# Half-width products: two PSUM sums in one bank, the second value mix in the freed one, and a new order of work

## The chip, the cores and the metric

One core of one Trainium2 chip. The metric is the device time of one execution in microseconds; lower is better. Three runs of the kernel before give a median of 2415.76 us (2412.73 to 2417.64).

## The reference

128 graphs ("batches") of 128 nodes with 512 features pass through two layers. Each ends in a residual and a layer norm without parameters (eps 1e-5).

```python
# layer 0: multi-head attention, 8 heads of 64, masked by the adjacency
q = inputs @ Wq + bq;  k = inputs @ Wk + bk;  v = inputs @ Wv + bv
logits = einsum('bqhd,bkhd->bhqk', q, k) / sqrt(64)
attn = softmax(where(adj > 0, logits, -1e9))
x = layernorm(x + relu(einsum('bhqk,bkhd->bqhd', attn, v) @ Wo + bo))
# layer 1: graph attention with one edge score per pair of nodes
Wh = x @ W;  e = leaky_relu((Wh @ a1)[:, :, None] + (Wh @ a2)[:, None, :], 0.2)
attention = softmax(where(adj == 0, -1e9, e), axis=2)
x = layernorm(x + elu(attention @ Wh))
```

Everything is float32. The value returned is x after layer 1, shape 128 x 128 x 512.

## The kernel before

**Tiling.** Batches are worked on in 64 pairs. The five big products are those with Wq and Wk (together "qk"), Wv ("v"), Wo ("o") and W ("w"). Each is done for a pair at once as a 2 x 2 block product with seven instead of eight block multiplications: the seven products of a family are numbered j = 0 to 6 in `PRODUCTS`, and each adds into one of three PSUM sums, A (j = 0, 2), B (j = 1, 3, 5) and C (j = 4, 6). This text writes A0 and A1, B5, B6 and B3, C4 and C7 for them, after the sum and the left block. Left blocks 4 to 7 are sums made by `left_sums` on POOL (`x_sums`, `o_sums`, `z_sums`; tiles sx, so, sz).

Between the products of one sum an engine reads it: after A0 comes `p1` (tile e1a or e1b), after A1 `c11`; after B5 `p6` (u2), after B6 `p7` (u3), after B3 `c21`; after C4 `c22`, after C7 `c12`. The next product into that sum waits for its reader. In v and w the readers of A are on ScalarE, all others of the half-width families on VectorE. The qk sums are 512 columns wide and fill a PSUM bank of 128 x 512 float32. The sums of v, o and w are 256 columns wide.

**PSUM.** Eight banks. The pool `ps_att` holds the logits of two batches, two banks each (tile s). The pool `ps_acc` has the tags accA, accB and accC, one bank each, which all four families use in turn; a half-width sum has a bank to itself and leaves half of it empty. The pool `ps` has one bank, for both value mixes of a pair (`mix_values`, tile po) and both node mixes (`mix_nodes`, tile pz), one after the other.

**The attention path of a batch**: logits (TensorE), `mask_logits` and `max_logits` (VectorE), `exp_logits` and `norm_logits` (ScalarE, eight instructions each), `weights_t` (VectorE transposes blocks of 32 into tile prb), `weights_out` and `weights_in` (to DRAM, tile prd, and back transposed, tile prT), `mix_values` (TensorE), `mix_values_out` (ScalarE, tile oT). The graph path: `edge_term` and `edge_blocks` (VectorE), `edge_row` (a DMA spreads a row over all partitions, tile ejr), `edge_sums` (ScalarE), `edge_leaky`, `edge_mask`, `edge_max` (VectorE), `edge_exp` (ScalarE), `edges_t` with its way through DRAM (atb, atd, attT), `mix_nodes`, then the w product, `elu_exp`, `elu_low`, `elu_max`, residual, norm, `store`.

**The order of the work** is written out: every step has a due time in `PLAN`, a pair adds `PERIOD`, `ENDS` adds a shift for the first three and the last four pairs, and all steps are issued in the order of the sums. Each engine runs its instructions in that order and waits where data or a buffer is not ready. `GOING` adds matmuls on the identity near the end, whose result nobody reads (`keep_going_late`).

```python
shift = ENDS.get(p if p < n_pair // 2 else p - n_pair, {}).get(key, 0.0)
events.append((p * PERIOD + PLAN[key] + shift, len(events), fn, args))
```

**The start.** Pair 0 uses plain products for qk (`qk_plain`). `weight_sums` makes the four summed weight blocks of each family (wqk and wv on VectorE, wo and w on POOL). `fold_a` multiplies W with a, so that the edge scores come straight from x; it loads each half of a as a_bc (256 KB, spread over the partitions) on POOL's queue when its turn comes, and `fold_t` and `fold_out` spread the result over the partitions.

**The end.** The last pair does o and w with plain products (`plain_product`), reloads the weight rows which the sums have overwritten (rows_o, rows_w), and transposes its softmax weights on TensorE (ppT, pat).

`BUFS` is the number of buffers of each SBUF tag.

Of the kernel before, what the change touches and what calls it, by code (L numbers as in the profile page):

```python
# [8 lines left out]
F32 = mybir.dt.float32  # L9
# [8 lines left out]
PERIOD = 78.768558  # L18
PLAN = dict(
    load_adj=-214.2762, load_blocks=-156.4567, sums_qk=-119.9046, x_transpose0=-118.9579, sums_v=-112.8775,  # L20
    x_transpose1=-64.055, sums_fold1=-60.5833, sums_fold_t1=-41.0724, sums_fold0=-37.6761, sums_fold_out1=-36.5398,
    qk0=-36.0224, x_sums=-35.8404, qk1=-32.9779, qk_p1=-31.7105, fill_logits0=-31.5232, sums_fold_t0=-29.2377,
    qk4=-28.6459, qk_p6=-28.5331, qk_p1q=-27.7049, qk2=-26.3155, qk_c11=-24.8916, qk3=-22.6254, v0=-21.402,
    qk_p7=-19.9439, qk_c22=-19.9339, qk5=-14.7467, qk6=-13.4439, qk_c21=-7.8856, qk_c12=-7.8498, v_p1=-4.7268,
    v1=-4.5449, fill_logits1=-1.8505, mask=-1.2435, v_p6=-0.2943, logits=0.0, sums_fold_out0=0.6684,
    mask_logits0=1.9952, max_logits0=3.7429, v3=4.4065, v_p7=4.433, v2=7.4467, v_c11=9.2069, v4=9.2085,
    mask_logits1=10.0374, load_x1=10.3213, v5=13.2871, v_c22=14.6665, exp_logits0=14.7511, v_c21=15.0921,
    v6=17.2266, v_c12=17.5754, max_logits1=22.1216, sums_o=22.3895, sum_logits0=24.0633, norm_logits0=27.409,
    exp_logits1=33.3029, weights_t0=43.7048, sum_logits1=43.7767, norm_logits1=52.0118, weights_out0=53.6197,
    weights_t1=55.6065, weights_out1=68.011, weights_in0=70.4393, weights_in1=74.301, mix_values0=75.8522,  # L30
    mix_values_out0=80.7212, mix_values1=81.4334, mix_values_out1=85.4398, load_x0=87.1711, sums_w=90.2554,
    o_sums=101.6394, o0=106.2181, o_p1=113.6365, o1=113.6652, o4=115.875, o_p6=116.2192, o_p1l=117.1503,
    o3=117.1603, o_p7=117.3205, o2=117.7709, o_c11=118.2449, o_c22=118.2872, o5=120.8539, o6=121.6955,
    o_c21=121.8792, residual01=122.7569, o_c12=122.7614, stats01=122.8191, mean01=123.8502, residual00=127.7304,
    rstd01=128.2803, shift01=128.7729, stats00=130.3078, norm01=131.2371, mean00=131.4538, rstd00=133.9815,
    edge_term01=134.3884, shift00=135.5918, edge_term11=137.3863, norm00=140.4496, edge_term10=144.2793,
    edge_blocks=146.1519, fill_edges=152.9599, edge_row=155.4786, edge_term00=159.9559, edge_sums=163.3873,
    edge_leaky=169.0665, edge_mask=174.9959, edge_max=179.2956, edge_exp=184.846, edges_t=185.9311,
    edges_t_out=188.282, edges_t_in=189.7663, mix_nodes1=211.95, mix_nodes_out1=218.2462, mix_nodes0=220.5122,
    mix_nodes_out0=222.7905, z_sums=231.0565, w0=248.2279, edge_norm=250.3865, w_p1=253.8429, w1=254.0225,  # L40
    w2=254.7456, w_p6=256.7486, w3=258.7144, w_c11=259.1252, w4=262.9461, w_p7=264.5461, w5=268.1992,
    w_c22=268.2862, w6=268.4953, w_c21=269.0061, w_c12=270.9016, elu_exp1=288.3615, elu_exp0=298.9658,
    elu_low1=307.1177, elu_max1=314.1197, elu_low0=326.1878, elu_max0=338.6625, residual10=340.2052,
    stats10=349.6362, mean10=349.9591, residual11=350.8328, rstd10=358.934, stats11=386.2458, mean11=395.8811,
    shift10=413.3316, rstd11=414.603, shift11=416.7025, finish0=436.5642, finish1=440.8676, store0=451.5942,
    store1=492.1186, tail_exp=492.2186, tail_max=492.3186, tail_sum=492.4186, tail_norm=492.5186)

ENDS = {
    0: dict(
        qk_p1=-693.3008, qk_p1q=-562.1962, qk_p6=-558.7086, qk0=-497.8592, x_transpose1=-494.0942,  # L50
        x_transpose0=-448.1221, fill_logits0=-367.3107, load_x1=-359.65, qk1=-335.4701, qk2=-331.5901,
        load_adj=-316.9328, load_blocks=-299.7933, qk_c11=-289.6601, tail_max=-280.732, mask=-257.6647, qk3=-220.34,
        fill_logits1=-212.9934, qk_c21=-211.3615, fill_edges=-182.6923, qk_c12=-180.0174, x_sums=-178.1562,
        logits=-170.7364, qk_c22=-165.6554, load_x0=-157.2757, qk5=-129.4956, exp_logits0=-115.2104,
        weights_out0=-114.1682, max_logits0=-113.2581, mask_logits1=-111.564, mask_logits0=-111.5243, v4=-108.9856,
        weights_t0=-107.8966, weights_in0=-106.3568, v1=-104.9602, v3=-103.5122, v_p6=-102.5092,
        sum_logits0=-99.1902, v_p1=-98.6495, v2=-98.1896, v_c22=-97.279, v_p7=-96.9685, v6=-95.93,
        max_logits1=-92.4852, v_c11=-92.0931, norm_logits0=-91.8454, v5=-91.0373, weights_t1=-89.8414, v0=-89.7163,
        norm_logits1=-87.923, sum_logits1=-87.4384, v_c12=-84.3643, exp_logits1=-84.0508, v_c21=-82.1213,
        weights_in1=-81.3671, weights_out1=-75.5973, mix_values0=-73.0572, o_sums=-72.5018,  # L60
        mix_values_out0=-71.3249, stats11=-70.0451, mix_values_out1=-68.3664, o0=-68.2642, mix_values1=-65.5116,
        o_p1l=-63.5095, o1=-61.1023, o_p1=-60.89, qk_p7=-54.0233, mean11=-52.6597, o2=-52.1908, o_p6=-51.8324,
        o3=-51.3338, o5=-49.9351, o_p7=-47.5345, o_c11=-46.8, o_c22=-46.5822, o6=-46.5728, residual11=-45.7167,
        o4=-45.2658, o_c21=-41.1905, store1=-37.7402, residual01=-37.493, elu_low0=-36.3281, residual00=-34.7161,
        stats01=-31.1527, stats00=-30.3568, o_c12=-30.2986, elu_low1=-29.8226, elu_exp0=-28.3417,
        edge_term10=-25.0922, norm00=-23.3134, mean00=-22.364, elu_exp1=-20.4366, elu_max1=-19.6739,
        shift00=-19.0277, rstd00=-18.0188, edge_max=-12.5663, edge_mask=-9.2627, edge_norm=-8.9206, mean01=-8.3685,
        w4=-8.2022, shift01=-8.0908, rstd01=-7.6618, mix_nodes1=-7.0678, edges_t=-6.1798, edge_exp=-5.696,
        edge_term00=-5.0867, edges_t_out=-4.9358, edge_leaky=-4.1925, mix_nodes0=-3.6711, mix_nodes_out1=-3.3264,
        w_c22=-2.764, w5=-2.6295, w6=-2.2085, w_p1=-1.9921, w_c21=-1.864, mix_nodes_out0=-1.4624, w_c12=-0.5349,  # L70
        w_p7=-0.4357, w1=-0.3674, edge_sums=-0.3649, finish1=-0.2784, edge_row=0.4769, w_p6=1.2165,
        edge_blocks=1.691, w_c11=1.7828, w3=2.1516, w0=2.4355, w2=2.5822, elu_max0=4.042, rstd11=4.5885,
        edge_term11=7.4074, norm01=8.5979, shift10=10.18, residual10=10.2246, edge_term01=10.4225, z_sums=13.5305,
        qk4=14.4327, edges_t_in=14.663, shift11=23.8601, stats10=33.5595, finish0=35.2453, store0=36.1082,
        rstd10=37.0667, mean10=39.7004, tail_exp=66.8184, tail_norm=66.9674, tail_sum=88.0048, qk6=88.4639),
    1: dict(
        tail_norm=-490.1808, tail_max=-153.045, load_x1=-116.7791, qk_p1q=-113.1873, qk0=-111.5532, qk_p1=-110.0434,
        qk4=-107.6095, qk2=-106.2391, qk3=-105.0977, x_sums=-102.7439, qk1=-102.1183, fill_logits0=-100.8075,
        qk_p6=-100.3165, qk_c11=-99.2056, qk_p7=-95.9145, v0=-95.2879, x_transpose1=-94.0568, v_p1=-93.2182,
        fill_logits1=-91.2167, qk5=-91.0325, qk_c22=-87.7854, qk_c21=-86.0555, mask=-83.9068, qk6=-74.9886,  # L80
        qk_c12=-72.8526, v1=-72.8444, max_logits1=-71.4972, v_p6=-70.6212, v4=-66.8154, v2=-66.3646,
        logits=-65.0664, mask_logits0=-65.0249, mask_logits1=-64.5572, v3=-63.432, exp_logits1=-63.0166,
        max_logits0=-62.096, v_c22=-61.3606, v_c11=-59.6449, v5=-58.7736, v_p7=-55.6045, elu_max0=-48.704,
        v6=-46.8286, v_c21=-46.2548, sum_logits0=-46.1168, residual10=-45.9116, elu_low0=-45.8965,
        exp_logits0=-45.0705, norm_logits0=-44.0432, v_c12=-37.6454, weights_in0=-36.7489, edge_norm=-35.6444,
# [150 lines left out]
BUFS = dict(  # L236
    xb=2, adj=5, xT=3, sx=1, pr=2, qT=2, kT=2, t=2, scr=1, cw=6, e1a256=1, mask=2, u2256=1, u3256=1, cv=2, x=3,
    prb=1, e1a512=1, e1b512=1, u2512=1, u3512=1, prT=2, oT=2, so=1, e1b256=1, co=6, at=1, ejr=1, e=1, atb=1, attT=1,
    zT=2, sz=1)


@with_exitstack
# [841 lines left out]
```

## Time and profile before

| | us |
|---|---|
| median of 3 runs | 2415.76 |
| the profiled execution | 2416.63 |
| its span, first to last instruction | 2414.8 |
| TensorE busy in the span | 2379.1 |
| VectorE / ScalarE / POOL busy | 1859.3 / 1557.8 / 1414.3 |
| granted TensorE clock, mean | 0.998 |

The span lies inside the execution's own time, 1.8 us below it. Busy times of one engine do not overlap with themselves, so span minus busy is what the engine stood idle. A group of matmuls overlaps its successor by its drain: the time it costs is from its start to the next start. One half product is four matmul records (two blocks, each in two passes), a qk product sixteen.

### The profile page before, as it was taken

To read this page: it belongs to the slowest core of one execution; us is meant where nothing else is said; L and a number is where in the kernel's file an instruction comes from. 1 tells how busy PE (TensorE), PEld (TensorE's weight loads), DVE (VectorE), ACT (ScalarE), POOL (GpSimd) and SP (SyncE) were. 2 spreads that over 40 slices of the span, in tenths; PEclk is the share of its full clock that TensorE was granted. 3 is DMA by queue.
4 is the path that set the end of the run, shared out by engine and by line. 5 is a ranking of instruction groups with operands and counts; after the bars stand their busy time and mean duration, and the time that the engine had idled before them with its cause. 6 is when DMAs were issued, how large, how long until landed. Compare 5 with 4: busy or idle time off the path is not lost.

```text
span 2414.8 us, 51884 instructions
## 1 busy us (share of the span) xinstructions
PE 2379.1 (99%) x17768; PEld 2147.7 (89%) x17768; DVE 1859.3 (77%) x3883; ACT 1557.8 (65%) x5512; POOL 1414.3 (59%) x1990
## 2 busy tenths in 40 slices
PE   8999999999999999999999999999999999999997
PEld 7889989989899899899899898998998998998885
DVE  5777777877877877777777778778778777777776
ACT  4656766766766666666667667666666666676664
POOL 3446665655556565665656555565566656555557
PEclk9999999999999999999999999999999999999999
DMA  8435445344344444454443443444444544534333
GB/s 194 114 67 130 112 105 131 101 118 123 104 123 116 112 123 115 101 134 109 108 132 101 117 123 103 123 117 112 123 115 101 134 110 108 134 98 116 109 85 81
DMA packets 341382, 276.59 MB, mean 115 GB/s; under 512 B 126400, under 2 KB 288960, under 8 KB 341120
## 3 DMA queue, kind: packets, MB, share of 16 engines
q1 hardware_dynamic: 339568, 271.17, 43.7%
q8 instruction: 142, 2.33, 0.4%
q10 hardware_dynamic: 1216, 1.31, 0.3%
q0 software_dynamic: 336, 0.79, 0.2%
q14 instruction: 120, 0.98, 0.1%
HBM read 156.90 MB, written 107.87 MB: 110 GB/s over the span
## 4 chain that ended last, share of the span: by engine, by line
PE 92%; DMA 3%; DVE 2%; ACT 2%; SPq 1%; issue 0%; POOL 0%; POOLq 0%; ACTq 0%; DVEq 0%
PE pBqk L486 14%; PE pCqk L486 9%; PE pAqk L486 9%; PE pBv L475 7%; PE pBo L475 7%; PE pBw L475 7%; PE po L804 5%; PE s L731 5%; PE pAo L475 4%; PE pz L914 4%; PE pCw L475 4%; PE pCo L475 4%; PE pAv L475 4%; PE pCv L475 4%; PE pAw L475 4%; DMA ejr<-ej 1%
## 5 line engine op out<-in xcount | busy, mean ns | idle before, releaser
L754 ACT ACTIVATE pr<-pr,nmax 128x128 f32<-128x128 f32 x1024 | 395.3, 390 | 4.0 <-DVE nmax L748 4.0
L763 ACT ACTIVATE pr<-pr,tot 128x128 f32<-128x128 f32 x1024 | 314.5, 411 | 49.8 <-DVE tot L758 49.6
L813 ACT ACTIVATE oT<-po,bv 128x128 f32<-128x128 f32 x512 | 145.0, 364 | 286.0 <-PE po L804 286.0
L956 POOL TENSOR_TENSOR cw<-cw,co 128x512 f32<-128x512 f32 x126 | 159.5, 1285 | 227.1 <-DVE cw L950 227.1
L513 POOL TENSOR_SCALAR rstd<-mv 128x1 f32<-128x1 f32 x255 | 97.6, 383 | 270.4 <-DVE mv L508 261.1
L945 POOL TENSOR_SCALAR t<-t 128x512 f32<-128x512 f32 x126 | 246.9, 1960 | 13.2 <-ACT t L941 13.1
L486 PE MATMUL pBqk<-sx,wqk 128*128 128x128 f32 x2016 | 245.6, 275 | 0.5 <-DVE tot L758 0.5
L486 PE MATMUL pCqk<-sx,wqk 128*128 128x128 f32 x2016 | 246.0, 275 | 0.0
L486 PE MATMUL pAqk<-xT,wqk 128*128 128x128 f32 x2016 | 245.5, 275 | 0.0
L486 PEld LDWEIGHTS pBqk<-sx,wqk 128*128 128x128 f32 x2016 | 239.8, 192 | 3.8 <-issue 0.6
L486 PEld LDWEIGHTS pAqk<-xT,wqk 128*128 128x128 f32 x2016 | 236.3, 192 | 7.0
L486 PEld LDWEIGHTS pCqk<-sx,wqk 128*128 128x128 f32 x2016 | 235.9, 192 | 0.2
L739 POOL MEMSET pr<- 128x1024 f32 x128 | 121.8, 953 | 134.4 <-DVE prb L773 129.8
L743 DVE COPY_PREDICATED pr<-mask,s 128x1024 f32<-128x1024 int32 x128 | 171.0, 1337 | 33.7 <-PE s L731 32.5
L835 DVE SCALAR_TENSOR_TENSOR scr<-co,wa_bc 128x512 f32<-128x512 f32 x256 | 186.3, 728 | 11.3 <-ACT co L523 5.7
L754 ACT ACTIVATION_READ_ACCUMULATOR pr<-pr,nmax 128x1 f32 x1024 | 193.8, 189 | 0.0
L773 DVE STREAM_TRANSPOSE prb<-pr 128x1024 f32<-128x1024 f32 x126 | 156.1, 1239 | 20.2 <-ACT pr L763 19.8
L514 POOL TENSOR_TENSOR rstd<-rstd,half 128x1 f32<-128x1 f32 x255 | 144.7, 567 | 21.2
L748 DVE TENSOR_REDUCE nmax<-pr 128x8 f32<-128x1024 f32 x128 | 155.3, 1213 | 0.2
L804 PE MATMUL po<-prT,cv 128*64 128x128 f32 x2048 | 140.2, 279 | 2.8 <-DMA prT<-prd 2.8
L919 ACT COPY zT<-pz 128x512 f32<-128x512 f32 x128 | 75.9, 593 | 100.8 <-PE pz L914 100.8
L475 PE MATMUL pBv<-wv,sx 128*128 128x256 f32 x512 | 138.0, 392 | 2.4 <-DVE u2v L679 1.3
(198 smaller groups left out, 5982.6 us busy)
## 6 DMA issues: line engine op xcount, KB each, us to landing
prd<-prb SPq DMA_DIRECT2D x126, 512.0 KB, 2.9
prT<-prd SPq DMA_DIRECT2D x504, 128.0 KB, 3.6
x<-in_x_dram SPq DMA_DIRECT2D x128, 256.0 KB, 4.2
out_dram<-cw SPq DMA_DIRECT2D x128, 256.0 KB, 3.6
xb<-in_x_dram SPq DMA_DIRECT2D x252, 128.0 KB, 4.0
adj<-in_adj_dram SPq DMA_DIRECT2D x64, 128.0 KB, 2.1
ejr<-ej SPq DMA_DIRECT2D x256, 32.0 KB, 3.9
atd<-atb SPq DMA_DIRECT2D x63, 128.0 KB, 1.8
```

What stands on the lines that cost most here:

```text
L475: nc.tensor.matmul(out, left_block(left, blk.pair, a_i, c), right_block(weight, b_i)[:, c, :], start=first and c == 0, stop=j in LAST and ...
L486: nc.tensor.matmul(out[:, f * P:(f + 1) * P], weight[:, b_i, c, f * P:(f + 1) * P], left_block(left, blk.pair, a_i, c), start=first and f ...
L743: nc.vector.copy_predicated(PR[b], MASK[p][:, i, :].unsqueeze(1).to_broadcast([P, H, P]), ST.pop(("s", b)).rearrange("p j h k -> p (j h) k"))
L748: nc.vector.tensor_reduce(NMAX[b], PR[b], AX.X, ALU.max, negate=True)
L754: nc.scalar.activation(PR[b][:, h, :], PR[b][:, h, :], AF.Exp, bias=nmax[:, h:h + 1], scale=1.0, accum_out=TOT[b][:, h:h + 1])
L763: nc.scalar.activation(PR[b][:, h, :], PR[b][:, h, :], AF.Copy, scale=tot[:, h:h + 1])
L773: nc.vector.transpose(PRB[b].rearrange("p k h s -> p h k s"), PR.pop(b).rearrange("p h (k r) -> p h k r", r=32))
L804: nc.tensor.matmul(ST["o", b][j * DH:(j + 1) * DH, hp, :], v[:, h * DH:(h + 1) * DH], prT[:, :, j * (H // 2) + hp, :], start=True, stop=True)
L813: nc.scalar.activation(OT[b][:, f, :], po[:, f, :], AF.Identity, bias=bv_sb[:, f:f + 1], scale=1.0)
L835: nc.vector.scalar_tensor_tensor(scr, X1[b], 1.0, wa_bc[s], op0=ALU.mult, op1=ALU.mult, accum_out=acc)
L945: side_engine(b // 2).tensor_scalar(t, t, 1.0, -1.0, op0=ALU.min, op1=ALU.add)
L956: side_engine(b // 2).tensor_tensor(Y[b], Y[b], X1.pop(b), op=ALU.add)
```

## The change

1. **PSUM.** For v and w the sums A and C become the two halves of one bank of tag accA, for o of tag accC (tile pAC). B keeps its bank. The value mix of the second batch of a pair takes a bank of tag accC instead of the bank of `ps`. In the last pair's plain o product the sum of the first batch moves to accC.
2. **a** is loaded whole, once, on SP's queue behind the loads of W, into a buffer of tag so; `fold_a` loads nothing.
3. **The plan.** All due times and PERIOD are new. `ENDS` and `GOING` are empty: all pairs have the same order, and the filler matmuls near the end are gone.
4. **Buffers.** adj 5 to 3, mask 2 to 1, x 3 to 2; e1a256 1 to 2, sz 1 to 2.
5. `qk_plain` keeps track of which sums have been started instead of relying on the order of its four steps.

```diff
-PERIOD = 78.768558
+PERIOD = 81.778385
 PLAN = dict(
...
-    0: dict(
...
-GOING = {('o3', -1): 6, ('mix_nodes0', -2): 2, ('w3', -2): 5, ('w5', -2): 10, ('edges_t', -1): 3, ('mix_nodes1', -1): 1}
+ENDS = {}
+
+GOING = {}
...
-    xb=2, adj=5, xT=3, sx=1, pr=2, qT=2, kT=2, t=2, scr=1, cw=6, e1a256=1, mask=2, u2256=1, u3256=1, cv=2, x=3,
+    xb=2, adj=3, xT=3, sx=1, pr=2, qT=2, kT=2, t=2, scr=1, cw=6, e1a256=2, mask=1, u2256=1, u3256=1, cv=2, x=2,
...
-    zT=2, sz=1)
+    zT=2, sz=2)
...
     load_rows(w_b, nc.sync, w)
+    a_bc = buf([P, 2, D], F32, "so", "a_bc")
+    nc.sync.dma_start(a_bc.rearrange("p i d -> p (i d)"), bass.AP(tensor=a.tensor, offset=a.offset, ap=[[0, P], [1, 2 * D]]))
...
     def fold_a(i):
-        a_bc = buf([P, D], F32, "t", f"a_bc{i}")
-        nc.gpsimd.dma_start(a_bc, bass.AP(tensor=a.tensor, offset=a.offset + i * D, ap=[[0, P], [1, D]]))
...
         def psum(self, bank):
+
             if bank not in self.bank:
-                self.bank[bank] = ps_acc.tile([P, self.width], F32, tag=f"acc{bank}", name=f"p{bank}{self.tag}_{self.name}")
+                if self.width == D or bank == "B":
+                    self.bank[bank] = ps_acc.tile([P, self.width], F32, tag=f"acc{bank}",
+                                                  name=f"p{bank}{self.tag}_{self.name}")
+                else:
+                    t = ps_acc.tile([P, D], F32, tag="accC" if self.tag == "o" else "accA",
+                                    name=f"pAC{self.tag}_{self.name}")
+                    self.bank["A"], self.bank["C"] = t[:, 0:HALF], t[:, HALF:D]
             return self.bank[bank]
...
-            b.bank[bank] = ps_acc.tile([P, D], F32, tag=f"acc{bank}", name=f"p{bank}{tag}_last")
+            b.bank[bank] = ps_acc.tile([P, D], F32, tag="accC" if tag + bank == "oA" else f"acc{bank}",
+                                       name=f"p{bank}{tag}_last")
...
     def mix_values(b):
         prT, v = PRT.pop(b), V.pop(b)
-        ST["o", b] = ps.tile([P, H // 2, P], F32, tag="ps", name=f"po_{b}")
+        pool, tag = (ps_acc, "accC") if b % 2 else (ps, "ps")
+        ST["o", b] = pool.tile([P, H // 2, P], F32, tag=tag, name=f"po_{b}")
```

The first product of a pair in a shared bank (A0) is the only one with the start flag; C4 has none, as sum C exists from then on.

The order on TensorE in the middle of the program, one period, from the logits on:

| before | logits of both batches, po of the second, B6 v, A1 v, C4 v, A0 w, B3 v, C7 v, B5 w, A1 w, B6 w, C4 w, A0 o, B3 w, C7 w, B5 o, C4 o, B6 o, A1 o, B3 o, A0 qk, C7 o, B5 qk, C4 qk, A1 qk, pz, B6 qk, A0 v, pz, B3 qk, C7 qk, B5 v, po of the first |
|---|---|
| after | logits of both batches, po of both, B6 v, C4 v, B3 v, C7 v, A0 o, A0 w, B5 w, A1 w, B6 w, C4 w, B3 w, C7 w, B5 o, C4 o, B6 o, A1 o, B3 o, A0 qk, C7 o, B5 qk, C4 qk, B6 qk, pz, A1 qk, B3 qk, A0 v, pz, C7 qk, B5 v, A1 v |

## The prediction

> **What bounds the kernel now.** I read the busy shares and the chain that ended last first, then the windows by stage, then TensorE's timeline in one steady period, at the start and at the end.
>
> ```profile
> PE 2379.1 (99%) x17768; PEld 2147.7 (89%) x17768; DVE 1859.3 (77%) x3883; ACT 1557.8 (65%) x5512; POOL 1414.3 (59%) x1990
> ...
> PE 92%; DMA 3%; DVE 2%; ACT 2%; SPq 1%; issue 0%; POOL 0%; POOLq 0%; ACTq 0%; DVEq 0%
> ```
>
> TensorE is busy for 2379.1 of 2414.8 us and carries 92% of the chain; 35.7 us are all that it is idle. The windows say where (columns: window, PE busy, PEld, DVE, ACT, POOL, clock, DMA share, GB/s):
>
> ```profile
> 0.00:50.00 50.00, 41.04 (x310) 38.38 (x311) 29.46 (x67) 22.26 (x82) 14.18 (x29) 0.96 0.83 198
> 50.00:100.00 50.00, 48.75 (x374) 43.68 (x374) 35.82 (x70) 28.14 (x111) 26.69 (x33) 0.97 0.43 109
> 100.00:150.00 50.00, 46.29 (x358) 42.51 (x357) 35.34 (x70) 31.56 (x120) 20.14 (x30) 1.00 0.40 96
> ...
> 1115.65:1152.40 36.75, 36.75 (x279) 33.33 (x278) 28.75 (x61) 24.27 (x86) 22.00 (x32) 1.00 0.45 116
> ...
> 2250.00:2300.00 50.00, 45.51 (x362) 40.32 (x362) 36.29 (x71) 26.12 (x92) 27.29 (x38) 1.00 0.45 119
> ...
> 2350.00:2415.00 65.00, 51.34 (x276) 37.83 (x274) 42.20 (x102) 32.77 (x77) 43.91 (x61) 0.97 0.31 82
> ```
>
> The middle has no idle time at all: the logits matmuls of pair 5 start at 197.23 and those of pair 60 at 2217.59, so a period is 2020.36/55 = 36.73 us. Idle time lies before 200 us (15.7) and after 2200 us (20.0). Hence three sums: start, 55 to 58 periods, end.
>
> A full PE does not mean that nothing can be lost in it. Two of its groups are longer than their neighbours. TensorE's timeline (start, us, operation):
>
> ```profile
> 1123.88 1.03 PE L475 MATMUL pBw<-w,sz 128*128 128x256 f32 x4
> 1124.74 1.03 PE L475 MATMUL pAw<-w,zT 128*128 128x256 f32 x4
> 1125.61 1.06 PE L475 MATMUL pBw<-w,sz 128*128 128x256 f32 x4
> 1126.51 1.03 PE L475 MATMUL pCw<-w,sz 128*128 128x256 f32 x4
> ```
>
> and VectorE's, the reader between the two pBw:
>
> ```profile
> 1125.00 0.42 DVE L679 TENSOR_TENSOR u2w<-pBw,e1aw 128x256 f32<-128x256 f32 x1 [0.50 <-PE pBw L475]
> ```
>
> A half product takes 0.865 us (start to start). One other product stands between two writes of a bank, so the reader must fit into 1.73 us: it starts 0.26 after the first product's last issue, takes 0.42, and the second pBw can go about 0.22 later. That is 0.865+0.26+0.42+0.22 = 1.765: the second group is 0.90 instead of 0.865, 0.035 lost. Where the matmul waits for one engine only, the release costs 0.15 after the reader's end (u3v ended at 2341.44; the product that waited for it started at 2341.49 and its group took 0.96, 0.10 over 0.865), and the fit is just met.
>
> **What the Trainium skill says.** "PSUM — Partial Sum Buffer", section "PSUM bank collisions raise a hardware error": semaphores must guard PSUM by bank (and 32-partition quadrant), not by address. So sums that share a bank exclude each other's writes and reads. Every sum of before has its own bank; its trace does not show this. "TensorE: Matmul & The Clock Gate", section "What's actually happening": after an idle window of about 3.4 us TensorE runs at half clock until it has been busy about as long. The trace agrees: after 4.14 us of idle at 43.8 the clock is 0.50 to 52.5.
>
> ```profile
> 47.95 1.09 PE L445 MATMUL pwa<-ident,wa_rep 128*128 128x128 f32 x4 [4.14 <-DVE wa_rep L439]
> 48.83 3.62 PE L486 MATMUL pBqk<-xT,wqk 128*128 128x128 f32 x16
> ...
> 49.50:51.00 1.50, 1.50 (x9) 1.50 (x9) 1.24 (x3) 0.16 (x1) 1.39 (x2) 0.50 0.40 164
> ```
>
> **The steady period.** The matmuls are the same, 278 instructions per period. In the built order the logits of both batches now stand together, then both value mixes, and each family of half products runs through on its own: B6 C4 B3 C7 of v; A0 of o; A0 B5 A1 B6 C4 B3 C7 of w; B5 C4 B6 A1 B3 of o. In the old order v, w and o were interleaved. I go through the period with the old durations.
>
> The second mix in accC: its bank was last read by c12 of qk (0.69 us), 4.7 us earlier on PE, and ACT copies it out (1.14) before A0 of o, 3.5 us later. No wait. One change of matmul shape falls away (mix between product and logits) and one comes (product to logits); 0.085 us seen at such a change. Zero net, between -0.1 and +0.1.
>
> Reuses with only one product between: six in the old order (two of them with two engines to wait for, 0.07 lost in all), ten in the new. Those with two engines are B6 and C7 of w, B6 of o: 3 x 0.035. In v, a 0.63 us transposition of x stands before c22 on VectorE, which then ends at 4.66 us after the logits, and C7 is due 4.75: with 0.15 for the release +0.05. The C4 of v and w now wait until ScalarE has read A (c11), the bank guard: c11 of w is read by 9.70, C4 is due at 10.03, no loss unless the eight exponentials ahead of it on ScalarE (3.1 us, done by 6.6) are late. New loss 0.17 minus old 0.07 = **+0.10 us a period**; bounds 0 (all readers in time) and +0.35 (each of ten late by 0.035, VectorE misplaced once more). 58 periods: **+6** (0 to +20).
>
> Buffers: a third x and the extra adj and mask buffers go. The load of x waits for the residual of two batches before and stands on SP ahead of the store of the second transposed weights; but in VectorE's order that residual precedes the transposition which that store needs, so SP waits for nothing new. The adj load waits for the edge mask (about 9.7) and is used at 32. SP's issues per period sum to some 15 of 36.7 us. Nothing; if a load were late, the value mix 3 us behind its weights would be next.
>
> **The start.** VectorE's order now has the sums of wv first, which cannot begin before the last wv piece lands (18.64+4.81 = 23.45), then mask, then the four sums of wqk (1.23 each). They end near 31.0 (before: 25.8 for all), and the first mask_logits follows at 31.4 instead of 25.70: +5.7. Against this, a rides on SP behind w (one 512 KB load instead of two of 256 KB on POOL's queue), so the 2.99 us that VectorE waited for a_bc and the 4.14 of PE go, and so does most of 2.2 us at half clock. The logits of pair 1 come at about 61 (56.36). The next two intervals equal the old ones to a microsecond (30 and 32). The two after that took 40.8 and 38.8 with old stalls at the mixes and at w (1.92 on prT, 1.79 on u2w, 1.75 on cv) and take 36.8 in the steady order: -6. Sum: **-1** (-6 to +5).
>
> **The end.** From pair 60's logits to pair 63's the old end order needs 2333.98-2217.59 = 116.4, with stalls such as
>
> ```profile
> 2262.81 1.13 PE L475 MATMUL pAw<-w,zT 128*128 128x256 f32 x4 [2.64 <-ACT cv L694]
> ```
>
> The steady order continued takes 3 x 36.83 = 110.5: **-6** (-6 to -3; x_sums of the last pair, four operations of 0.4 on VectorE, stand before c11 of o and are hidden behind qk's A0).
>
> After that the old end takes 2414.8-2333.98 = 80.8. In the new order the last pair's o sum waits, on PE, behind w of pair 61, whose B3 needs u3w, which on VectorE stands behind the edge row of pair 62 (ejr, 3.9 us on its way). Followed through, the last edge transposition comes at 60 after the logits' end (old 59.5), the last product ends at 71.6 (70.7): +1. The 54 filler matmuls (7.0 us of PE, L998) are gone:
>
> ```profile
> 2391.03 2.39 PE L998 MATMUL keep_going<-ident 128*128 128x128 f32 x20
> ```
>
> PE then stands for 3 us and again for about 6, and some 9 us of products after it run at half clock until it recovers: estimate +4.5 (0 to +7, from the 2.2 lost at 48). Such walks miss small waits: +1.5. Sum **+7** (-3 to +13).
>
> **Sum.** +6-1-6+7 = +6 on the profiled execution's 2416.63 (span 2414.8). It stands 0.87 above the median of the runs; against that, 2415.76+6 = **2422 us**.
>
> **Rivals.** (1) *Faster*: the old end shifts are the stalls, and dropping them costs nothing. For: 6.7 of the 20 us of late idle are between pairs 60 and 62. If readers always fit (0) and the tail is +1 without clock loss: 0-1-6+1 = -6, **2410**. Against: the fillers and B3's wait. It decides if the period stays below 36.78. (2) *Slower by more*: VectorE is the second bound inside a family: 0.865 per product against 0.33 to 0.42 per reader and whatever the order puts between. If it loses 0.35 a period: 20-1-6+7, **2436**. For: 77% busy; against: most readers have 0.3 us spare in the walk. (3) *It does not do what it says*: the freed bank is handed on at once, the bank guard puts back what it saves, and the ends cancel: **2416**.
>
> **How the numbers follow.** 0.2% (4.8 us) is about what a measurement of this kernel can tell from no change. Main case 0.50 (0.12 of it within the bound), rival 1 0.24 (0.02 within), rival 2 0.17, rival 3 0.09 (within). Faster 0.22, same 0.23, slower 0.55. The range leaves out the fast edge of rival 1 and the far side of rival 2: 2406 to 2437.
>
> **What would show it.** Right: a period of 36.8 to 36.9 with 0.90 instead of 0.865 at B6 and C7; no 4.14 at pwa; mask_logits first near 31; PEclk below 1.0 in the last 40 us. Wrong: a period of 36.73 or less, or above 37; a stall at po after s (prT late); a tail under 79 us.

## The result and the profile after

The changed kernel takes **2436.77 us** (median of 4 runs, 2435.75 to 2437.97) against 2415.51 for the kernel before (4 runs): 1.0089 times, 95% interval 1.0071 to 1.0106. The forecast was 2422 in a range of 2406 to 2437: the time lies at the upper edge of the range, the sign was right, the size was not, +21 instead of +6. The time lies where rival 2 (VectorE is the second bound, 2436) had put it.

The logits matmuls of a pair mark the stages:

| stage | before | after | difference | forecast |
|---|---|---|---|---|
| start, to the logits of pair 5 | 197.23 | 194.73 | -2.5 | -1 |
| pair 5 to pair 60 (55 periods) | 2020.36 | 2043.49 | +23.1 | +5.5 |
| pair 60 to pair 63 | 116.39 | 111.45 | -4.9 | -6 |
| last logits to the end | 80.8 | 86.5 | +5.7 | +7 |
| span | 2414.8 | 2436.2 | +21.4 | +6 |

Three of the four terms lie in their ranges. The steady period went from 36.73 to 37.15 us, +0.42 where +0.10 stood; a period above 37 was among the prediction's own signs of being wrong. The page of the changed kernel, busy times and then the chain that ended last:

```profile
PE 2387.2 (98%) x17714; PEld 2142.7 (88%) x17714; DVE 1913.5 (79%) x3883; ACT 1571.4 (65%) x5512; POOL 1496.6 (61%) x1988
...
PE 72%; POOL 7%; DVE 6%; DMA 6%; issue 4%; ACT 3%; SPq 2%; ACTq 0%; POOLq 0%; DVEq 0%
```

Apart from the fillers the matmuls are the same, but TensorE carries 72% of the chain instead of 92%, and POOL, which had none of it, carries 7%. VectorE is busy for 54 us more and POOL for 82 us more, with as many instructions as before (3883; 1988 for 1990): they have become longer. The windows by stage (PE, PEld, DVE, ACT, POOL, clock, DMA share, GB/s):

```profile
50.00:100.00 50.00, 47.27 (x375) 42.30 (x376) 35.73 (x67) 29.71 (x118) 24.60 (x33) 0.99 0.52 122
100.00:150.00 50.00, 50.00 (x376) 46.15 (x375) 35.59 (x72) 31.38 (x118) 22.60 (x32) 0.98 0.42 104
1123.57:1160.72 37.15, 36.90 (x277) 33.26 (x276) 29.68 (x61) 24.50 (x86) 23.42 (x32) 1.00 0.46 114
2250.00:2300.00 50.00, 49.76 (x357) 44.81 (x355) 38.85 (x85) 35.10 (x127) 30.95 (x41) 1.00 0.43 109
2350.00:2436.20 86.20, 63.16 (x330) 46.92 (x326) 55.28 (x124) 42.68 (x121) 52.49 (x71) 0.89 0.29 72
```

The old stalls at 100 to 150 and 2250 to 2300 us are nearly gone. In their place each middle period, which had no idle time, now has 0.25 us of it. TensorE's timeline shows where:

```profile
1123.57 2.06 PE L558 MATMUL s<-kT,qT 64*128 64x128 f32 x32
1125.55 1.97 PE L632 MATMUL po<-prT,cv 128*64 128x128 f32 x32
1127.45 1.13 PE L298 MATMUL pBv<-wv,sx 128*128 128x256 f32 x4
1128.42 1.03 PE L298 MATMUL pACv<-wv,sx 128*128 128x256 f32 x4
1129.69 1.13 PE L298 MATMUL pBv<-wv,xT 128*128 128x256 f32 x4 [0.25 <-DVE u3v L528]
1130.66 1.09 PE L298 MATMUL pACv<-wv,sx 128*128 128x256 f32 x4
1131.58 1.03 PE L298 MATMUL pACo<-wo,oT 128*128 128x256 f32 x4
```

From start to start: C4 to B3 takes 1.27 instead of 0.865 (+0.405: the wait, the drain before it and the start after it), B3 to C7 0.97 (+0.105), C7 to A0 of o 0.92 (+0.055). Together **+0.57 a period, all of it in v**. What B3 waits for, on VectorE:

```profile
1122.87 1.14 DVE L663 SCALAR_TENSOR_TENSOR scr<-co,wa_bc 128x512 f32<-128x512 f32 x1
...
1124.27 1.41 DVE L663 SCALAR_TENSOR_TENSOR scr<-co,wa_bc 128x512 f32<-128x512 f32 x1
...
1125.61 2.60 DVE L570 COPY_PREDICATED pr<-mask,s 128x1024 f32<-128x1024 int32 x2
1128.10 1.21 DVE L575 TENSOR_REDUCE nmax<-pr 128x8 f32<-128x1024 f32 x1
1129.22 0.42 DVE L528 TENSOR_TENSOR u3v<-pBv,e1av 128x256 f32<-128x256 f32 x1
...
1130.17 0.39 DVE L533 TENSOR_TENSOR cv<-pACv,u3v 128x256 f32<-128x256 f32 x1
```

VectorE works without a pause. u3v, which empties B for B3, stands behind both mask_logits and the first maximum. These stand behind two edge terms (scr) of the pair two before, which take 1.14 and 1.41 us where the same instruction takes 0.69 elsewhere. Beside them POOL runs

```profile
1121.57 1.20 POOL L198 TENSOR_TENSOR sz<-zT,zT 128x256 f32<-128x256 f32 x1
1122.73 0.73 POOL L199 TENSOR_TENSOR sz<-zT,sz 128x256 f32<-128x256 f32 x1
1123.41 3.40 POOL L784 TENSOR_TENSOR cw<-cw,co 128x512 f32<-128x512 f32 x2
```

and is slowed too: a residual takes 1.70 us against 1.25 in the kernel before. The Trainium skill, page "SBUF — State Buffer", section "SBUF: two separate sides", gives a reason: VectorE, when an operation has two inputs in SBUF, and GpSimd (POOL here), when it reads SBUF, share a pair of ports as an exclusive lock, held for the whole instruction. The trace fits to about 0.15 us: the first scr is issued at 1122.87, 0.59 before POOL's sz ends at 1123.46, and ends at 1124.01, as if it had begun at about 1123.3. The first residual, issued at 1123.41, has half of the pair's 3.40 us and ends near 1125.1, where 1.25 us from 1124.01 on would make 1125.26. The second scr, issued at 1124.27, ends at 1125.68, 0.6 after that. The lock does not show beside every POOL instruction: in the kernel before, two edge terms that run beside a tensor_scalar of POOL (tile t, 1141.81 to 1143.76) take 0.83 and 0.69. What the control and the experiments below show is the effect of the neighbours; the lock is the page's reason for it. The chain of waits (start, us, what) tells the same:

```profile
1123.46 3.37 POOL cw L784 x2
...
1126.87 1.33 DVE pr L570
1128.21 0.47 DVE nmax L575
1128.68 0.54 issue
1129.22 0.43 DVE u3v L528
...
1129.69 1.13 PE pBv L298 x4
```

The start of the program holds a control. In pair 3 (logits at 121.01) no residual runs yet, the second scr takes 0.68 (the first, beside sz, still 1.14), B3 does not wait, and the interval to pair 4 is 36.58 us.

### The profile page after: what moved, and what is told of

It is laid out like the page before. It is cut to its first block, busy times and chain, and to the rows that moved or that the text cites. A ratio compares the mean times of both kernels' runs of the same rounds, so it can differ in the third digit from the quotient of the medians.

```text
span 2436.2 us, 52003 instructions
## 1 busy us (share of the span) xinstructions
PE 2387.2 (98%) x17714; PEld 2142.7 (88%) x17714; DVE 1913.5 (79%) x3883; ACT 1571.4 (65%) x5512; POOL 1496.6 (61%) x1988
## 3 DMA queue, kind: packets, MB, share of 16 engines
q10 hardware_dynamic: 1216, 1.31, 0.3%
## 4 chain that ended last, share of the span: by engine, by line
PE 72%; POOL 7%; DVE 6%; DMA 6%; issue 4%; ACT 3%; SPq 2%; ACTq 0%; POOLq 0%; DVEq 0%
PE pBqk L309 14%; PE pAqk L309 9%; PE pACw L298 9%; PE pACo L298 9%; PE pBw L298 7%; PE pBo L298 7%; PE pACv L298 5%; PE pCqk L309 5%; POOL cw L784 5%; PE pz L742 5%; PE pBv L298 3%; DMA ejr<-ej 2%; SPq L676 2%; DMA x<-in_x_dram 2%; DVE pr L570 2%
## 5 line engine op out<-in xcount | busy, mean ns | idle before, releaser
L336 POOL TENSOR_SCALAR rstd<-mv 128x1 f32<-128x1 f32 x255 | 105.4, 413 | 372.7 <-DVE mv L331 360.0
L663 DVE SCALAR_TENSOR_TENSOR scr<-co,wa_bc 128x512 f32<-128x512 f32 x256 | 248.9, 972 | 94.3 <-ACT co L346 94.1
L784 POOL TENSOR_TENSOR cw<-cw,co 128x512 f32<-128x512 f32 x126 | 212.6, 1708 | 0.9 <-DVE cw L778 0.9
L570 DVE COPY_PREDICATED pr<-mask,s 128x1024 f32<-128x1024 int32 x128 | 165.7, 1349 | 2.2 <-PE s L558 2.1
L197 POOL TENSOR_TENSOR sz<-sz,zT 128x256 f32<-128x256 f32 x63 | 46.0, 731 | 167.3 <-ACT zT L747 167.2
L558 PEld LDWEIGHTS s<-kT,qT 64*128 64x128 f32 x2048 | 119.3, 188 | 21.2 <-issue 20.6
```

Of the source, the lines that this page charges most:

```text
L570: nc.vector.copy_predicated(PR[b], MASK[p][:, i, :].unsqueeze(1).to_broadcast([P, H, P]), ST.pop(("s", b)).rearrange("p j h k -> p (j h) k"))
L663: nc.vector.scalar_tensor_tensor(scr, X1[b], 1.0, wa_bc[s], op0=ALU.mult, op1=ALU.mult, accum_out=acc)
L784: side_engine(b // 2).tensor_tensor(Y[b], Y[b], X1.pop(b), op=ALU.add)
```

## The experiments

Theory A: VectorE's run of work between the logits and v's readers is too long, for two reasons: its order, and the edge terms slowed by POOL. Rivals: the bank that A and C share (B), the order on VectorE alone (C), the place of u3v alone (D). e1, e2, e5 and e7 were timed against the kernel before (4 to 6 runs each); e3, e4, e6 and e8 are one run each, read from their profiles.

**e1: one edge term earlier on VectorE.**

```diff
-    edge_term01=169.2474
+    edge_term01=157.6
```

> One VectorE instruction of another pair (edge_term of the second batch, scr, 1.14 us) is moved from between c12 of qk and u2v to the place where VectorE stands idle for 1.51 us waiting for the norm; nothing else moves. Theory A (VectorE's run of work in front of v's readers is too long: scr 1.14 and 1.41, both mask_logits 2.60, max 1.21, then u3v): mask_logits starts about 0.9 us earlier, u3v ends before B3 of v is due, the 0.25 us wait at B3 goes, the period falls from 37.15 to 36.55-36.65 and the time to about 2404 us (2400 to 2409). Rival B (it is the bank that A and C share, or the short distance between two products of one sum): nothing changes, 37.15 and 2437 us.

Measured: **2402.48 us** (2400.19 to 2405.05), 0.9939 times the kernel before in the same comparison (2417.52; interval 0.9919 to 0.9958). Period 36.58. VectorE:

```profile
1104.51 0.69 DVE L663 SCALAR_TENSOR_TENSOR scr<-co,wa_bc 128x512 f32<-128x512 f32 x1
...
1107.72 0.78 DVE L663 SCALAR_TENSOR_TENSOR scr<-co,wa_bc 128x512 f32<-128x512 f32 x1
...
1109.34 2.58 DVE L570 COPY_PREDICATED pr<-mask,s 128x1024 f32<-128x1024 int32 x2 [0.83 <-PE s L558]
...
1113.12 0.42 DVE L528 TENSOR_TENSOR u3v<-pBv,e1av 128x256 f32<-128x256 f32 x1
```

The logits start at 1108.07 here: mask_logits comes 1.27 us after that instead of 2.04, and now VectorE waits 0.83 us for TensorE. The moved term takes 0.69 instead of 1.14, since POOL is idle at its new place; the other takes 0.78, since it is now ahead of the residual. TensorE waits nowhere between 300 and 2200 us. Theory A holds, and rival B falls for the steady period: banks and products are as in the changed kernel.

**e2: the residuals later on POOL.**

```diff
-    residual10=323.2556, residual11=327.6948
+    residual10=338.4, residual11=338.5
```

> Only POOL's order changes: the two residuals of layer 1 (1.72 us each in the changed kernel) go behind o_sums, so that they no longer run beside the edge terms on VectorE. Theory A with its second part (the edge terms take 1.14 and 1.41 us instead of 0.69 because POOL works beside them): scr is 0.7 again, mask_logits starts 0.7 to 0.9 us earlier, period 36.55-36.70, time 2403-2411 us, VectorE's instructions in the same order as before the edit. Rival C (only the order on VectorE counts, POOL does not matter): period 37.15, 2437 us. If POOL's later residual holds up the statistics behind it, a new wait shows at u2w and the period is 36.9-37.1.

Measured: 2409.70 us, 0.9967 (0.9955 to 0.9979), period 36.73, a little above the expected 36.55 to 36.70. VectorE:

```profile
1111.65 1.14 DVE L663 SCALAR_TENSOR_TENSOR scr<-co,wa_bc 128x512 f32<-128x512 f32 x1
...
1113.05 0.67 DVE L663 SCALAR_TENSOR_TENSOR scr<-co,wa_bc 128x512 f32<-128x512 f32 x1
...
1113.66 2.59 DVE L570 COPY_PREDICATED pr<-mask,s 128x1024 f32<-128x1024 int32 x2
```

The second term, with no residual beside it, is back at 0.67; the first still meets sz and stays at 1.14. That is enough: mask_logits starts 1.31 us after the logits and v has no wait. So POOL alone, without any move on VectorE, makes and unmakes the stall: rival C falls. The residual at its new place holds the statistics by 0.65 us, u2w with them, and B6 of w loses 0.14: hence 36.73 and not 36.58.

**e3: u3v ahead of the maximum.**

```diff
-    v_p7=13.5346
+    v_p7=12.8
```

> u3v goes ahead of max_logits on VectorE, all else in place. Theory A (the sum of VectorE's work up to c22 of v decides): the 0.25 us wait at B3 goes, but c22 now ends some 0.4 us later, since VectorE waits for B6 first, and C7 of v waits 0.7-0.9 us instead: period 37.3-37.6, no gain, 2445-2462 us. Rival D (only u3v's own place behind max costs the time): period 36.55-36.75, 2403-2412 us.

Measured: 2472.81 us, period 37.70, a little above the range of theory A. TensorE:

```profile
1107.99 1.03 PE L298 MATMUL pBv<-wv,xT 128*128 128x256 f32 x4
1109.86 1.13 PE L298 MATMUL pACv<-wv,sx 128*128 128x256 f32 x4 [0.84 <-DVE cv L533]
```

B3 comes at once, and C7 waits 0.84 us for c22: VectorE now waits 0.42 us for B6, and c22 ends 5.55 us after the logits' end instead of 5.0. Rival D falls: it is not one reader's place that costs the time but the sum of VectorE's work up to c22.

**e4: both mixes in one bank again.**

```diff
-        pool, tag = (ps_acc, "accC") if b % 2 else (ps, "ps")
+        pool, tag = (ps, "ps")
```

> The second value mix goes back to the bank of the first; the sums A and C stay in one bank and the order stays. Theory: the second mix, which now follows the first at once, waits for ScalarE's copy of the first (1.14 us and its way there and back): 1.2 to 1.6 us of wait at po in every period, while the wait at B3 of v goes because VectorE catches up; period 37.7-38.2, 2470-2500 us. Rival: the copy is hidden by something else, or the time is absorbed by the old wait: 37.1-37.3, 2434-2446 us.

Measured: 2498.26 us, period 38.05. TensorE:

```profile
1117.95 1.09 PE L632 MATMUL po<-prT,cv 128*64 128x128 f32 x16 [1.24 <-ACT oT L641]
```

The second mix waits for the copy of the first; in exchange v has no wait. The freed bank is what lets the mixes follow each other: without it the same order costs 0.90 us a period more.

**e8: e1, and the first mix ahead of the logits again.**

```diff
-    mix_values0=88.5416, weights_in0=82.6464
+    mix_values0=81.76, weights_in0=81.7
```

> The edit of e1, and the first value mix goes ahead of the logits on TensorE, where the kernel before had it; no other engine's order changes. Theory: two things are lost. The two mixes apart take one change of matmul shape more (2.05 instead of 1.90 us for both), +0.15; and B6 and B3 of v come 0.87 us sooner after the logits, so that u3v, which ends 5.3 us after the logits' start, is late again by some 0.6 us at B3 with 0.1 at the restart: period 37.3-37.6, 2447-2464 us. Rival: the place of the mixes costs only the change of shape: period 36.73, 2411-2413 us.

Measured: 2451.65 us, period 37.40. TensorE:

```profile
1131.64 1.09 PE L632 MATMUL po<-prT,cv 128*64 128x128 f32 x16
1132.67 2.06 PE L558 MATMUL s<-kT,qT 64*128 64x128 f32 x32
1134.65 1.09 PE L632 MATMUL po<-prT,cv 128*64 128x128 f32 x16
1135.68 1.13 PE L298 MATMUL pBv<-wv,sx 128*128 128x256 f32 x4
1136.65 1.03 PE L298 MATMUL pACv<-wv,sx 128*128 128x256 f32 x4
1137.99 1.13 PE L298 MATMUL pBv<-wv,xT 128*128 128x256 f32 x4 [0.32 <-DVE u3v L528]
```

Mix, logits, mix take 4.04 us to B6, against 3.88 in e1: 0.16 for one more change of shape. And B3 is late again (1.34 after C4), because the readers of v now come 0.87 us sooner after the logits' start. The joined mixes are also the cover under which VectorE masks the logits.

**e6: a as before**, loaded by fold_a on POOL's queue instead of by SP behind w:

```diff
+        a_bc = buf([P, D], F32, "t", f"a_bc{i}")
+        nc.gpsimd.dma_start(a_bc, bass.AP(tensor=a.tensor, offset=a.offset + i * D, ap=[[0, P], [1, D]]))
```

> The changed kernel with a loaded as in the kernel before: 256 KB for each half on POOL's queue when fold_a has its turn. Theory from the prediction: VectorE waits for a_bc again (2.99 us in the kernel before) ahead of fold_a, TensorE waits longer at B6 of qk or pwa, and the logits of pair 1 come 2-3 us after the 57.3 of the changed kernel; time +2 to +3, 2439-2440 us. Rival: POOL has issued the loads long before VectorE gets there and nothing changes: 57-58 us, 2436-2438.

Measured: 2437.87 us. VectorE does not wait for a_bc, so this part of the theory fails: the load of the second half is issued at 39.9 and VectorE comes to it at 45.39, 5.5 us later (36.5 and about 40.45 in the kernel before, where the load took 7.0; here it took 5.1 at most). The longest stall of the start is the same 3.00 us in both (here in e6's timeline), at B6 of qk behind fold_a:

```profile
45.62 2.89 PE L309 MATMUL pBqk<-sx,wqk 128*128 128x128 f32 x16 [3.00 <-DVE u2qk L409]
```

Pair 1's logits still come at 58.93 instead of 57.26, and pair 2's 1.67 us late too (88.12 for 86.45). This comes from earlier: the sums of wv wait longer for their weights (they start at 19.67 and 23.35 instead of 18.46 and 21.46). In e1, e2, e5 and e7, with a on SP and the same order up to there, pair 1's logits lie between 56.43 and 58.61, so this one run does not tell what the load's place is worth. That the logits of pair 5 are level again (194.77 for 194.73) says nothing about it: from pair 2 to pair 3 the changed kernel lost 1.6 us to the half clock (last section), and e6 did not.

**e5 and e7: the end.** e5 is e1 with filler matmuls behind the last node mix of pair 62; e7 is e1 with the last edge row issued behind w of pair 62.

```diff
-GOING = {}
+GOING = {('mix_nodes0', -2): 24}
```

> The edit of e1 (edge_term of the second batch earlier), and 24 matmuls on the identity behind the last node mix of pair 62, where TensorE stood idle for 3.85 us and then ran w of pair 62 at half clock. If the half clock is what the end lost against the kernel before: B5 of w is held by z_sums at the same time as in e1, but B5, A1 and B6 take 0.87 to 1.0 instead of 1.9, 1.9 and 1.4 us; the stretch from the last logits to the end falls from 83.6 to 81-82 us, time about 2400.5 (2399 to 2402). Rival: the readers of w on ScalarE and VectorE set the pace there and PE waits longer instead: 83-84 us, 2402-2404.

```diff
-ENDS = {}
+ENDS = {-1: dict(edge_sums=5.0, edge_leaky=9.5, edge_mask=9.0, edge_max=4.6, edge_exp=4.0)}
```

> The edit of e1, and in the last pair alone the row of edge scores (edge_sums on ScalarE; edge_leaky, edge_mask, edge_max on VectorE) is issued behind c11 and c22 of w of pair 62 instead of ahead of them. Theory (at the end the engines' order counts, not the clock: c11 and u3w of pair 62 stand behind the edge row of pair 63, which lands late): C4 of w starts about 2 us earlier, w of pair 62 is done before the edge row, pat follows the edge exponential at once, and the stretch from the last logits to the end falls by 1.0-1.3 us, from 83.6 to 82.3-82.6; time about 2401.3 (2400 to 2402.5). Rival: the last edge row itself, then pz and the plain w product set the end, and w of pair 62 is beside it: 83.4-83.7 us, 2402.5.

Measured: e5 2402.88 us (0.9941, 0.9925 to 0.9958), e7 2402.81 (0.9942, 0.9924 to 0.9960): neither differs from e1. From the last logits to the end e1 takes 83.6 us, e5 86.0, e7 84.7; in these profiled executions the starts of e5 and e7, up to pair 1's logits, were 1.0 and 1.4 us shorter than e1's, which hides part of it in the totals. e5's timeline of TensorE:

```profile
2361.15 5.52 PE L826 MATMUL keep_going<-ident 128*128 128x128 f32 x48
...
2372.07 1.10 PE L298 MATMUL pBw<-w,sz 128*128 128x256 f32 x4 [2.18 <-DVE u2w L506]
2375.17 2.08 PE L298 MATMUL pACw<-w,sz 128*128 128x256 f32 x4 [1.99 <-ACT cw L521]
2377.03 1.91 PE L298 MATMUL pBw<-w,zT 128*128 128x256 f32 x4
```

The fillers were longer than meant (each matmul is two records), but B5, B6 and C4 of w start within 0.1 us of e1's times counted from the last logits. The readers set the pace, as the rival said; the idle time then lies later, and C4, B3 and C7 get the half clock instead. In e7 C4 no longer waits for the edge row and starts 1.2 us sooner (2 were expected), and pat starts 0.9 us sooner as meant; then the half clock falls on what follows:

```profile
2377.00 0.71 PE L719 MATMUL pat<-ident,at 128*128 128x128 f32 x2 [0.66 <-ACT at L704]
...
2380.08 1.79 PE L742 MATMUL pz<-attT,co 128*128 128x128 f32 x8 [0.68 <-ACT zT L747]
2381.66 2.97 PE L480 MATMUL pAw_last<-rows_w,zT 128*128 128x512 f32 x4
```

pz takes 0.6 us and the first plain product 1.1 us longer than in e1, more than was won. Both expectations of a gain failed: at this end idle time is moved, not removed.

**Not tried**: the new order in the old banks, and the old order in the new ones. The new order puts A0 of w straight behind A0 of o; with both in accA the second would wait for a release that comes only after later products of o. The old order starts w before v's sum C is finished, which a bank shared by A and C excludes. So banks and order are one change; this is argued from the order of the work, not run.

## Why the prediction was wrong in size

**The steady period.** The forecast of +0.10 had three terms; this is what each measured.

- *"One change of matmul shape falls away ... and one comes ... Zero net."* A miscount: product, mix, logits, mix, product are four changes, product, logits, mixes, product are three. Logits and both mixes took 4.03 us from start to start (1.03, 1.98, 1.02) and take 3.88 (1.98, 1.90): **-0.15**, which e8 gives back.
- *"Those with two engines are B6 and C7 of w, B6 of o."* B6 and C7 of w did become 0.90 (1135.04 to 1135.94, 1137.67 to 1138.57), B6 of o stayed at 0.865. The kernel before had two groups of 0.90 as well: **0**, not +0.10. In the steady period no wait shows at any C4, so the guard of a shared bank cost nothing there, as forecast; at the end C4 does wait (below).
- *"In v, a 0.63 us transposition of x stands before c22 on VectorE, which then ends at 4.66 us after the logits, and C7 is due 4.75"*: **+0.57** instead of +0.05, and this is the step that failed. In the trace c22 ends 5.0 us after the logits' end (1125.55), and u3v, at which the prediction counted no loss, ends at 4.1 where B3 was due at 3.74.

The reason stands in the prediction's own sentence, *"I go through the period with the old durations."* The durations were not the kernel's to keep: the new order moved POOL's sums and residuals beside the edge terms, and two instructions of 0.69 became 1.14 and 1.41, +1.17 us in a walk in which most readers had 0.3 to spare. Undoing part of this by either engine (e1, e2) removes the whole stall. Without it the new order is better than the old by 0.15 a period. Rival 2 named VectorE and the right size, 0.35 against 0.42 measured; it was given 0.17, with the spare time counted without what the neighbours do to it. That its sum came so close is in part luck: it had 19.3 us for the 55 periods where 23.1 were measured, and the other three terms took 1.7 of the difference back.

**The start** was in its range for partly wrong reasons. The wait of 4.14 at pwa went (0.68 is left), but a stall of 3.00 at B6 of qk came behind fold_a, with the half clock behind it again (3.57 us for that product instead of 1.95), and e6, in which VectorE does not wait for a either, shows that the load on SP was not needed to end that wait. mask_logits came at 28.67, not 31.4: the sums of wv began at 18.46 with the first pieces, where the prediction let them all wait for the last. At 97.42 came a wait of 1.64, for VectorE's e1bo, that was not foreseen. It stands in all the experiments (1.51 to 1.75 us), but in the changed kernel's profiled execution alone the half clock followed it: from pair 2 to pair 3 that one takes 34.56 us, and e1, e2, e5, e6 and e7 take 32.93 or 32.94. So without these 1.6 us, which no experiment loses there, the -2.5 of the start would be about -4.

**The end** was in its range as a sum: -4.9 and +5.7 for -6 and +7. The -4.9 is three periods of 37.15 where 36.83 was forecast, the same stall. The two nearly cancel: from pair 60's logits to the last instruction the kernel before takes 197.2 us and the changed one 198.0, so the end without the end shifts and the fillers costs 0.8 us with the stall in it; in e1, without the stall, it takes 193.3. As forecast, the half clock came back:

```profile
2401.27 2.08 PE L298 MATMUL pACw<-w,zT 128*128 128x256 f32 x4 [3.85 <-ACT zT L747]
...
2411.40 2.08 PE L298 MATMUL pACw<-w,sz 128*128 128x256 f32 x4 [2.06 <-ACT cw L521]
```

Six products of w run at half clock and take some 5 us of TensorE more than at full clock. By e5, where the first three ran at full clock and the next began no sooner, only the three from C4 on can lie on the path. From C4's start to pat they take 5.15 us, and 3.3 in e1, where they run at full clock: about 1.9 of the 4.5 that were forecast. The second line also shows what was not forecast, the guard of the shared bank: C4 waits 2.06 us until ScalarE has read A (c11), which stands there behind edge_sums, and that waits for the last edge row, 4.4 us on its way. In the kernel before, C4 had a bank of its own and started right behind A1. What else makes up the +5.7 is left open.

## What to carry to other kernels

When an order changes, list for every stretch on the critical path what runs beside it on the engine that shares its memory ports, and price it with that neighbour: a duration from the old profile belongs to the old neighbours. A stall of a saturated engine can be cured two engines away: here a residual on POOL slowed an edge term on VectorE, which delayed a mask, a maximum and a reader, and TensorE paid; moving one instruction of 1.14 us into an idle gap made the kernel some 34 us faster than the changed one and 0.6% faster than the one before. If a reader is late, count all the work up to the last reader of the family before moving the first (e3).

## What the hardware showed that was not expected

The half clock came after far less than one long idle stretch, and not every time. In the changed kernel's profiled execution TensorE was busy for 1.51 of 3.40 us, with waits of 1.64 and 0.33, and then ran at half clock for 2.8 us (windows as above):

```profile
95.40:98.80 3.40, 1.51 (x6) 0.68 (x4) 2.79 (x9) 1.98 (x9) 0.32 (x2) 1.00 0.13 39
98.80:101.60 2.80, 2.72 (x7) 2.21 (x8) 0.76 (x3) 2.80 (x13) 2.72 (x4) 0.50 0.23 58
```

In e1 the same products wait 1.65 and 0.33 us, TensorE is busy for the same 1.51 of 3.40, and the clock stays at full, as it does at this place in the other seven experiments:

```profile
96.00:99.40 3.40, 1.51 (x6) 0.68 (x4) 2.79 (x9) 1.97 (x9) 0.31 (x2) 1.00 0.14 40
99.40:102.20 2.80, 2.71 (x13) 2.43 (x14) 1.48 (x5) 2.80 (x13) 2.72 (x5) 1.00 0.22 58
```

So neither the longest wait nor the busy share of such a stretch decides alone. The Trainium skill, page "TensorE: Matmul & The Clock Gate", section "What's actually happening", calls the window in which the activity is watched free-running. Then it would matter where a wait falls in the window, which would fit; no run here shows the window itself.
